# Turning the adjacency with the DMA engines instead of TensorE, through a bf16 copy in DRAM

## The chip, the cores and the metric

The kernel runs on one core of a Trainium2 chip. The metric is device time in microseconds (us) of one execution. All times are medians of 4 executions, except for the kernel before: it ran 4 times to compare with the changed kernel (3 of them were known before the prediction) and 7 times beside each group of experiments.

## The reference, cut to what matters

Sixteen batches of 1024 nodes with 256 features go through four graph attention layers. Every layer of a batch uses the same adjacency, an int32 matrix of 1024 x 1024.

```python
_a = jax.random.bernoulli(key, 0.00390625, (16, 1024, 1024))
_a = jnp.logical_or(_a, jnp.swapaxes(_a, -1, -2))     # symmetric
adj = jnp.logical_or(_a, jnp.eye(1024, dtype=bool)).astype(jnp.int32)
# simplified; each layer:  h = max(layernorm(x), 0)
#              x = x + attention(h, adj)    softmax over j, masked where adj[i, j] == 0
```

The inputs are symmetric, but the reference does not promise it, so the kernel turns each block of adjacency. An unturned block still gives the right result here.

## The kernel before

The kernel keeps a turned uint8 mask of each batch in SBUF, the memory that all engines work in; TensorE writes its results to PSUM, from where another engine copies them. `load(b)` fetches it, 128 rows at a time. It is a generator: the program calls it step by step, one block after each of eight groups of layer 3 of batch b-2.

```python
    def load(b: int):
        xs[b] = nodes.tile([P, NI, D], F32, name="x_b")
        nc.sync.dma_start(xs[b], x[b].rearrange("(i p) f -> p i f", p=P))
        mask = masks[b] = nodes.tile([P, NI, N], U8, name="mask")
        fetched = {}

        def fetch(i: int):
            fetched[i] = adjs.tile([P, N], BF, name="adj_i")        # 3 buffers
            nc.gpsimd.dma_start(fetched[i], adj[b, ts(i, P), :])    # casts int32 to bf16
        for i in range(AHEAD):                                      # AHEAD = 2
            fetch(i)
        yield
        for i in range(NI):                                         # NI = 8
            if i + AHEAD < NI:
                fetch(i + AHEAD)
            adj_i = fetched.pop(i)
            every = wide.tile([P, N], BF, name="wide")
            nc.scalar.activation(                                   # a check of the values
                every, adj_i, AF.Square, bias=minus_half, accum_out=squares[:, b, i : i + 1]
            )
            turned = psum.tile([P, NI, P], BF, name="misc", bufs=3)
            for j in range(NI):
                nc.tensor.transpose(turned[:, j, :], adj_i[:, ts(j, P)], ident_b)
            nc.scalar.copy(mask[:, :, ts(i, P)], turned)
            yield
    ...
    def batch(b: int):
        ...
        coming = load(b + 2) if b + 2 < B else iter(())
        ...
        V = yield from attend(0, V, finish0, 1)      # layer 0, projecting for layer 1
        V = yield from attend(1, V, finish, 2)
        V3 = yield from attend(2, V, finish, 3)
        ...
        for n in range(H * NH):                      # layer 3: 8 groups
            ...
            nc.scalar.copy(sums, accT)
            next(coming, None)                       # one block of batch b + 2
            ...
```

Two streams of batches, even and odd, run half a batch apart. A scheduler then orders the instructions of each engine with a simulation of its own, so the order on an engine is not the order of the program. `tc.keep_in_program_order(ins)` keeps an instruction behind everything that the program gave its engine earlier. Each engine works through its built order without overtaking.

Of the kernel before, what the change touches and what calls it, by code (L numbers as in the profile page):

```python
# [33 lines left out]
BF = mybir.dt.bfloat16  # L34
# [7 lines left out]
P = 128  # L42
# [17 lines left out]
def short_path(ctx: ExitStack, tc: tile.TileContext, ins: dict, out: bass.AP, bad: bass.AP):  # L60

    nc = tc.nc
    x, adj = ins["x"], ins["adj"]
    B, N, D = x.shape
    H, T, E = ins["L3_a_src"].shape
    NI = N // P
# [10 lines left out]
    adjs = ctx.enter_context(tc.tile_pool(name="adjs", bufs=3))  # L77
    wide = ctx.enter_context(tc.tile_pool(name="wide", bufs=2))
    psum = ctx.enter_context(tc.tile_pool(name="psum", bufs=2, space=bass.MemoryType.PSUM))

    ident = const.tile([P, P], F32, name="ident")
    make_identity(nc, ident)
    ident_b = const.tile([P, P], BF, name="ident_b")
# [8 lines left out]


    xs, masks = {}, {}

    def load(b: int):

        xs[b] = nodes.tile([P, NI, D], F32, name="x_b")
        nc.sync.dma_start(xs[b], x[b].rearrange("(i p) f -> p i f", p=P))
        mask = masks[b] = nodes.tile([P, NI, N], U8, name="mask")  # L100
        fetched = {}

        def fetch(i: int):

            fetched[i] = adjs.tile([P, N], BF, name="adj_i")
            nc.gpsimd.dma_start(fetched[i], adj[b, ts(i, P), :])  # L106

        for i in range(AHEAD):
            fetch(i)
        yield  # L110
        for i in range(NI):
# [5 lines that stand above are left out]
            nc.scalar.activation(  # L117
                every, adj_i, AF.Square, bias=minus_half, accum_out=squares[:, b, i : i + 1]
            )
            turned = psum.tile([P, NI, P], BF, name="misc", bufs=3)  # L120
            for j in range(NI):
                nc.tensor.transpose(turned[:, j, :], adj_i[:, ts(j, P)], ident_b)  # L122
            nc.scalar.copy(mask[:, :, ts(i, P)], turned)
            yield

    edges = ctx.enter_context(tc.tile_pool(name="edges", bufs=4))
# [104 lines left out]
    def project(l: int, xb: bass.AP, pair: int, evict):  # L231


        mv = small.tile([P, 2, nc.vector.BN_AGGR_DIM], F32, name="mv")
        for n in range(2):
            stats = small.tile([P, nc.vector.BN_STATS_DIM], F32, name="stats")
            nc.vector.bn_stats(stats, xb[:, 2 * pair + n, :])  # L237
            nc.vector.bn_aggr(mv[:, n, :], stats)
        rstd = inverse_root(mv[:, :, 1], 2, LN_EPS)
        centered = work.tile([P, 2, D], F32, name="centered", bufs=3)  # L240
        for n in range(2):
            nc.vector.tensor_scalar(  # L242
                centered[:, n, :], xb[:, 2 * pair + n, :], mv[:, n, 0:1], 0.0,
                op0=ALU.subtract, op1=ALU.max,
            )
        yield 0.5
        turned = psum.tile([P, NK, 2 * P], F32, name="misc", bufs=3)
        for n in range(2):
            for k in range(NK):
                nc.tensor.transpose(turned[:, k, ts(n, P)], centered[:, n, ts(k, P)], ident)  # L250
        hT = wide.tile([P, NK, 2 * P], F32, name="hT", bufs=3)
        nc.scalar.copy(hT, turned)  # L252
        yield 1.0
        for n in range(2):
            projected = psum.tile([P, D + EXT[l]], F32, name="projected")
            for k in range(NK):
                nc.tensor.matmul(  # L257
                    projected, hT[:, k, ts(n, P)], W[l][:, k, :],
                    start=(k == 0), stop=(k == NK - 1),
                )  # L260
            evict(2 * pair + n, projected, rstd[:, n : n + 1])
        yield 2.5

    def weigh(column, c, mask: bass.AP, op, half: int, into: list):


        turned = psum.tile([P, HALF], F32, name="misc", bufs=3)
        for n in range(NG):
            nc.tensor.transpose(  # L269
                turned[:, ts(n, P)], column(half * NG + n).to_broadcast([P, P]), ident  # L270
            )
        r = rows.tile([P, HALF], F32, name="row")
        nc.scalar.copy(r, turned)  # L273
        w = edges.tile([P, NI, HALF], F32, name="weights")
        into.append(w)
        for j in range(NI):
            nc.vector.scalar_tensor_tensor(  # L277
                w[:, j, :], r, c(j), mask[:, j, ts(half, HALF)], op0=op, op1=ALU.mult
            )
            if j % 4 == 3:  # L280
                yield 1.5
# [17 lines left out]
    def batch(b: int):  # L299
        xb, mask = xs.pop(b), masks.pop(b)  # L300
        if b == 0:
            next(preparing)
        coming = load(b + 2) if b + 2 < B else iter(())

        def begin(l: int):

            V = nodes.tile([P, NI, H, E + 1], F32, name="V").rearrange("p i h e -> p i (h e)")

            def evict(i: int, projected: bass.AP, rstd: bass.AP):
                nc.scalar.activation(V[:, i, D : D + 3], projected[:, D:], AF.Exp, scale=rstd)  # L310
                if l == 2:
                    nc.scalar.mul(V[:, i, :D], projected[:, :D], rstd)
                else:
                    nc.vector.tensor_scalar(  # L314
                        V[:, i, :D], projected[:, :D], rstd, V[:, i, D : D + 1],
                        op0=ALU.mult, op1=ALU.mult,
                    )

            return V, evict

# [3 lines left out]
        def begin3():  # L324
            h3 = last["h3"] = single.tile([P, NI, D], F32, name="h3")
            V3 = nodes.tile([P, NI, H, E + 1], F32, name="V")
            ex = last["ex"] = small.tile([P, NI, 3 * H], F32, name="ex", bufs=2)

            def evict3(i: int, projected: bass.AP, rstd: bass.AP):
                nc.scalar.activation(ex[:, i, :], projected[:, D:], AF.Exp, scale=rstd)  # L330
                nc.scalar.mul(h3[:, i, :], projected[:, :D], rstd)
                q = ex[:, i, :H].unsqueeze(2)
                nc.gpsimd.tensor_mul(
                    V3[:, i, :, :E], h3[:, i, :].rearrange("p (h e) -> p h e", h=H),
                    q.to_broadcast([P, H, E]),
                )
                nc.gpsimd.tensor_copy(V3[:, i, :, E:], q)
                nc.gpsimd.tensor_add(xb[:, i, :], xb[:, i, :], beta)

            return V3, evict3  # L340

        def attend(l: int, V: bass.AP, finish, then: int):

            op = ALU.min if l == 1 else ALU.max
            halves = []
            weighing = [
                weigh(
                    lambda i: V[:, i, D + 2 : D + 3], lambda j: V[:, j, D + 1 : D + 2],
                    mask, op, half, halves,
                )  # L350
                for half in range(NH)
            ]
            yield from weighing[0]
            following = begin(then) if then < 3 else begin3()
            steps = iter(())
            for i in range(NI):
                t = next(weighing[1], None)
                if t:
                    yield t
                acc = psum.tile([P, HALF], F32, name="acc", bufs=3)[:, : D + 1]  # L360
                w = halves[i // NG]
                for j in range(NI):
                    nc.tensor.matmul(  # L363
                        acc, w[:, j, ts(i % NG, P)], V[:, j, : D + 1],
                        start=(j == 0), stop=(j == NI - 1),
                    )
                finish(i, acc)
                yield 3.6
                if i % 2 == 1:

                    yield from steps
                    steps = project(then, xb, i // 2, following[1])
                yield from islice(steps, 1)
            yield 1.0
            yield from steps
            return following[0]
# [8 lines left out]
        def finish(i: int, acc: bass.AP):  # L385
            add_elu(xb[:, i, :], acc)
# [10 lines left out]
                pass  # L397
        V = yield from attend(0, V, finish0, 1)
        V = yield from attend(1, V, finish, 2)
        V3 = yield from attend(2, V, finish, 3)  # L400


# [37 lines left out]
        for n in range(H * NH):  # L440
# [5 lines left out]
            for j in range(NI):  # L446
                nc.tensor.matmul(  # L447
                    accT, V3[:, j, h, :], w[:, j, :], start=(j == 0), stop=(j == NI - 1)
                )
# [29 lines left out]
    def stream(first: int):  # L479
# [3 lines left out]
        for b in range(first, B, 2):  # L483
            yield from batch(b)

    loading, preparing = load(0), prepare()
    next(loading)
    next(preparing)
    streams = [[0.0, stream(0)], [LAG, stream(1)]]
# [384 lines left out]
```

## Time and profile before

| | before |
|---|---|
| time, median of 3 (range) | 3267.69 us (3262.37 to 3269.32) |
| span of the profiled execution | 3263.2 us |
| TensorE busy, idle | 3075.4 us, 187.8 us |
| VectorE, ScalarE, GpSimd busy | 2546.2, 969.4, 1085.1 us |
| granted TensorE clock, mean | 0.986 |

"Busy" of an engine is the time covered by its instructions; idle is the span less that. TensorE is the bound: it idles 5.8% of the span. The lines behind the table stand in the prediction, with their reading. A group's line there has line, engine, operation, shapes and count, then busy us and mean ns of one, then the idle time before it and what ended that. A wait's line has who waited, for what, then us in total, times and the longest.

### The profile page before, as it was taken

To read this page: it belongs to the slowest core of one execution; us is meant where nothing else is said; L and a number is where in the kernel's file an instruction comes from. 1 tells how busy PE (TensorE), PEld (TensorE's weight loads), DVE (VectorE), ACT (ScalarE), POOL (GpSimd) and SP (SyncE) were. 2 spreads that over 40 slices of the span, in tenths; PEclk is the share of its full clock that TensorE was granted. 3 is DMA by queue.
4 is the path that set the end of the run, shared out by engine and by line. 5 is a ranking of instruction groups with operands and counts; after the bars stand their busy time and mean duration, and the time that the engine had idled before them with its cause. 6 is when DMAs were issued, how large, how long until landed. Compare 5 with 4: busy or idle time off the path is not lost.

```text
span 3263.2 us, 38469 instructions
## 1 busy us (share of the span) xinstructions
PE 3075.4 (94%) x13702; PEld 2130.8 (65%) x13702; DVE 2546.2 (78%) x6140; ACT 969.4 (30%) x2081; POOL 1085.1 (33%) x1286
## 2 busy tenths in 40 slices
PE   7999999999999999999999999999999999999987
PEld 6765766657666676666766567675676766767562
DVE  5778787777887778877788877888778777787867
ACT  3423323232332323323233232322323223232121
POOL 1323424233242332423334233342323424233242
PEclk8999999999999999999999999999999999999999
DMA  4101101011010111100111010110101101000000
GB/s 105 27 4 17 33 14 39 7 17 30 14 39 7 17 30 17 36 11 13 30 17 36 10 21 23 16 36 13 39 4 17 33 13 40 4 14 13 1 13 14
DMA packets 55958, 72.13 MB, mean 22 GB/s; under 512 B 5072, under 2 KB 38992, under 8 KB 55760
## 3 DMA queue, kind: packets, MB, share of 16 engines
q0 software_dynamic: 18432, 33.56, 7.1%
q1 hardware_dynamic: 37328, 36.05, 3.6%
q8 instruction: 110, 1.80, 0.2%
q14 instruction: 88, 0.72, 0.1%
HBM read 86.38 MB, written 16.78 MB: 32 GB/s over the span
## 4 chain that ended last, share of the span: by engine, by line
PE 71%; DVE 17%; POOL 6%; issue 3%; ACT 2%; DMA 1%; POOLq 0%; ACTq 0%; SPq 0%; DVEq 0%
PE acc L363 32%; PE acc L447 22%; PE projected L257 11%; DVE weights L277 7%; PE misc L250 2%; PE misc L269 2%; POOL x_b L297 2%; DVE centered L242 2%; DVE stats L237 2%; POOL rstd L228 1%; PE misc L122 1%; DVE above L295 1%; DVE above L296 1%; POOL y L427 1%; ACT below L293 1%
## 5 line engine op out<-in xcount | busy, mean ns | idle before, releaser
L363 PE MATMUL acc<-V,weights 128*128 128x257 f32 x6144 | 1444.7, 385 | 9.5 <-DVE weights L277 8.1
L363 PEld LDWEIGHTS acc<-V,weights 128*128 128x128 f32 x6144 | 1142.9, 191 | 207.2 <-DVE weights L277 39.6
L447 PE MATMUL acc<-weights,V 128*65 128x512 f32 x2048 | 909.6, 592 | 0.3 <-DVE weights L277 0.3
L277 DVE SCALAR_TENSOR_TENSOR weights<-row,ex,mask 128x512 f32<-128x512 f32 x1024 | 744.5, 775 | 36.5 <-ACT row L273 36.5
L277 DVE SCALAR_TENSOR_TENSOR weights<-row,V,mask 128x512 f32<-128x512 f32 x768 | 593.0, 814 | 49.5 <-ACT row L273 48.1
L228 POOL TENSOR_TENSOR rstd<-rstd,minus_half 128x2 f32<-128x2 f32 (+1 forms) x320 | 330.4, 1035 | 882.4 <-DVE rstd L227 834.0
L447 PEld LDWEIGHTS acc<-weights,V 128*65 128x65 f32 x2048 | 278.7, 138 | 497.1 <-issue 475.5
L257 PE MATMUL projected<-W,hT 128*128 128x259 f32 (+1 forms) x2048 | 522.1, 397 | 40.6 <-DVE V L314 24.7
L257 PEld LDWEIGHTS projected<-W,hT 128*128 128x128 f32 x2048 | 387.4, 195 | 135.6 <-DVE V L314 37.0
L297 POOL TENSOR_TENSOR x_b<-x_b,above 128x256 f32<-128x256 f32 x256 | 222.0, 867 | 478.2 <-DVE above L296 440.7
L293 ACT ACTIVATE below<-acc,inv 128x256 f32<-128x256 f32 x256 | 121.0, 473 | 657.3 <-DVE inv L286 460.8
L237 DVE BATCH_NORM_STATS2 stats<-x_b 128x6 f32<-128x256 f32 x512 | 209.1, 415 | 128.4 <-POOL x_b L297 120.5
L250 PE MATMUL misc<-ident,centered 128*128 128x128 f32 x1024 | 168.9, 281 | 89.6 <-DVE centered L242 76.3
L252 ACT COPY hT<-misc 128x512 f32<-128x512 f32 x256 | 147.2, 588 | 302.4 <-PE misc L250 301.6
L242 DVE TENSOR_SCALAR centered<-x_b,mv 128x256 f32<-128x256 f32 x512 | 229.4, 451 | 4.7
L451 ACT COPY sums<-acc 65x512 f32<-65x512 f32 x128 | 74.1, 579 | 511.4 <-PE acc L447 509.9
L250 PEld LDWEIGHTS misc<-ident,centered 128*128 128x128 f32 x1024 | 120.5, 143 | 143.0 <-DVE centered L242 114.2
L273 ACT COPY row<-misc 128x512 f32<-128x512 f32 x224 | 129.8, 587 | 197.5 <-PE misc L269 197.3
L106 POOL DMA_DIRECT2D adj_i<-in_adj_dram x128 | 77.6, 606 | 284.9 <-ACT sums L451 215.4
L295 DVE TENSOR_SCALAR above<-acc,inv 128x256 f32<-128x256 f32 x256 | 122.6, 479 | 62.1 <-ACT below L293 60.9
L412 POOL TENSOR_TENSOR y<-y,bias 128x512 f32<-128x512 f32 x64 | 90.2, 1410 | 234.0 <-DVE y L459 215.7
L310 ACT ACTIVATE V<-projected,rstd 128x3 f32<-128x3 f32 x384 | 99.1, 262 | 226.0 <-PE projected L257 226.0
(70 smaller groups left out, 2307.8 us busy)
## 6 DMA issues: line engine op xcount, KB each, us to landing
adj_i<-in_adj_dram POOLq DMA_DIRECT2D x128, 256.0 KB, 3.8
x_b<-in_x_dram SPq DMA_DIRECT2D x16, 1024.0 KB, 7.8
out_dram<-y SPq DMA_DIRECT2D x32, 512.0 KB, 3.8
W<-in_L_gnn_W_dram SPq DMA_DIRECT2D x3, 256.0 KB, 9.6
weights<-in_L_gnn_a_dram SPq DMA_DIRECT2D x3, 256.0 KB, 9.6
W<-in_L_gnn_W_dram SPq DMA_DIRECT2D x2, 128.0 KB, 10.3
weights<-in_L_gnn_a_src_dram SPq DMA_DIRECT2D x1, 128.0 KB, 8.8
weights<-in_L_gnn_a_dst_dram SPq DMA_DIRECT2D x1, 128.0 KB, 5.2
```

Source lines behind the costliest of these rows:

```text
L228: nc.gpsimd.tensor_tensor(r, r, minus_half.to_broadcast([P, n]), op=ALU.pow)
L237: nc.vector.bn_stats(stats, xb[:, 2 * pair + n, :])
L242: nc.vector.tensor_scalar(centered[:, n, :], xb[:, 2 * pair + n, :], mv[:, n, 0:1], 0.0, op0=ALU.subtract, op1=ALU.max,)
L250: nc.tensor.transpose(turned[:, k, ts(n, P)], centered[:, n, ts(k, P)], ident)
L252: nc.scalar.copy(hT, turned)
L257: nc.tensor.matmul(projected, hT[:, k, ts(n, P)], W[l][:, k, :], start=(k == 0), stop=(k == NK - 1),)
L277: nc.vector.scalar_tensor_tensor(w[:, j, :], r, c(j), mask[:, j, ts(half, HALF)], op0=op, op1=ALU.mult)
L293: nc.scalar.activation(below, acc[:, :D], AF.Exp, scale=inv)
L295: nc.vector.tensor_scalar(above, acc[:, :D], inv, 0.0, op0=ALU.mult, op1=ALU.max)
L297: nc.gpsimd.tensor_add(xi, xi, above)
L363: nc.tensor.matmul(acc, w[:, j, ts(i % NG, P)], V[:, j, : D + 1], start=(j == 0), stop=(j == NI - 1),)
L447: nc.tensor.matmul(accT, V3[:, j, h, :], w[:, j, :], start=(j == 0), stop=(j == NI - 1))
```

## The change

The intent is to take the turning from TensorE. For batches 2 to 15, four casting transfers on GpSimd write the whole matrix as bf16 to a scratch in DRAM. The program issues them before layer 2 of batch b-2, and holds them in program order on GpSimd. In layer 3, Sync loads each block with a transposing DMA, and ScalarE copies it straight from SBUF into the mask. The first two batches stay as they were.

```diff
+    narrows = [dram.tile([N, N], BF, name=f"narrow{n}") for n in range(2)]
     def load(b: int):
+        by_dma = b >= 2
+        if by_dma:
+            for q in range(4):
+                quarter = ts(q, N // 4)
+                cast = nc.gpsimd.dma_start(narrows[b % 2][quarter, :], adj[b, quarter, :])
+                tc.keep_in_program_order(cast)
+        yield
 ...
-            nc.gpsimd.dma_start(fetched[i], adj[b, ts(i, P), :])
+            if by_dma:
+                nc.sync.dma_start_transpose(fetched[i], narrows[b % 2][:, ts(i, P)])
+            else:
+                nc.gpsimd.dma_start(fetched[i], adj[b, ts(i, P), :])
 ...
-            turned = psum.tile([P, NI, P], BF, name="misc", bufs=3)
-            for j in range(NI):
-                nc.tensor.transpose(turned[:, j, :], adj_i[:, ts(j, P)], ident_b)
-            nc.scalar.copy(mask[:, :, ts(i, P)], turned)
+            if by_dma:
+                nc.scalar.copy(mask[:, i, :], adj_i)
+            else:
+                (the four lines above)
 ...
         V = yield from attend(1, V, finish, 2)
+        next(coming, None)
         V3 = yield from attend(2, V, finish, 3)
```

More of the change, by code (lines that the diff above doesn't have):

```diff
@@ L79, in short_path @@
     psum = ctx.enter_context(tc.tile_pool(name="psum", bufs=2, space=bass.MemoryType.PSUM))
+    dram = ctx.enter_context(tc.tile_pool(name="dram", bufs=1, space=bass.MemoryType.DRAM))
     ident = const.tile([P, P], F32, name="ident")
@@ L119, in load @@
             )
-            turned = psum.tile([P, NI, P], BF, name="misc", bufs=3)
-            for j in range(NI):
-                nc.tensor.transpose(turned[:, j, :], adj_i[:, ts(j, P)], ident_b)
-            nc.scalar.copy(mask[:, :, ts(i, P)], turned)
+            if by_dma:
+                nc.scalar.copy(mask[:, i, :], adj_i)
+            else:
+                turned = psum.tile([P, NI, P], BF, name="misc", bufs=3)
+                for j in range(NI):
+                    nc.tensor.transpose(turned[:, j, :], adj_i[:, ts(j, P)], ident_b)
+                nc.scalar.copy(mask[:, :, ts(i, P)], turned)
             yield
@@ L486, in short_path @@
     loading, preparing = load(0), prepare()
+    next(loading)
     next(loading)
```

## The prediction

> **What bounds the kernel now.** I read the busy shares first, then the windows of one period, then TensorE's timeline, then the waits. The times before are 3262 to 3269 us, median 3267.69.
>
> ```profile
> PE 3075.4 (94%) x13702; PEld 2130.8 (65%) x13702; DVE 2546.2 (78%) x6140; ACT 969.4 (30%) x2081; POOL 1085.1 (33%) x1286
> q0 software_dynamic: 18432, 33.56, 7.1%
> ```
>
> TensorE is busy 94% of the span and VectorE 78%; ScalarE and the DMA engines are mostly idle. Two batches are in flight, half a batch apart, so stores of `y` leave every 200 us. The windows (busy us of TensorE, its weight loads, VectorE, ScalarE, GpSimd, then granted clock) of two such periods:
>
> ```profile
> 1556.00:1756.00 200.00, 192.87 (x864) 133.55 (x865) 161.38 (x394) 60.86 (x131) 73.31 (x88) 1.00 0.11 23
> 1756.00:1957.00 201.00, 190.36 (x850) 131.92 (x848) 156.61 (x369) 59.85 (x130) 63.64 (x73) 0.99 0.11 21
> ```
>
> TensorE idles 7 to 11 us of each 200, at full clock. It sets the period, so the work taken from it is worth nearly its issue time, and any wait put into its order costs nearly its length.
>
> The timeline around two groups of eight turning transposes (L122), columns start, duration, engine, line:
>
> ```profile
> 1628.06 7.03 PE L447 MATMUL acc<-weights,V 128*65 128x512 f32 x16
> 1634.93 0.61 PE L122 MATMUL misc<-ident_b,adj_i 128*128 128x128 bf16 x8
> 1635.37 0.61 PE L250 MATMUL misc<-ident,centered 128*128 128x128 f32 x4
> 1635.82 0.60 PE L269 MATMUL misc<-ident,V 128*128 128x128 f32 x4
> 1636.67 0.46 PE L456 MATMUL misc<-ident,sums 65*128 65x65 f32 x4 [0.26 <-ACT mask L123]
> ...
> 1650.90 0.61 PE L122 MATMUL misc<-ident_b,adj_i 128*128 128x128 bf16 x8
> 1651.35 0.87 PE L363 MATMUL acc<-V,weights 128*128 128x257 f32 x3
> ```
>
> From the start of a group to the start of the next work it is 0.44 to 0.45 us: eight times 55 ns. The duration of 0.61 us overlaps what follows, so the busy sum overstates the cost. The groups by shape and the waits:
>
> ```profile
> L122 PE MATMUL misc<-ident_b,adj_i 128*128 128x128 bf16 x1024 | 79.9, 222 | 9.9 <-DMA adj_i<-in_adj_dram 7.5 <-ACT mask L123 1.9
> L123 ACT CAST mask<-misc 128x1024 uint8<-128x1024 bf16 x128 | 129.0, 1011 | 1.5 <-PE misc L122 1.4
> PE misc L456 <- ACT mask L123: 11.7, 14, 1.4
> POOL adj_i L106 <- ACT sums L451: 215.4, 51, 14.8
> ```
>
> The third line: fourteen times (once a batch) L456 waits for a PSUM buffer that still holds a turned block. The fourth: GpSimd's in-order queue stands 215 us before a load, because a buffer is not free; this rarely ends TensorE's idle time.
>
> **What the Trainium skill says.** "TensorE: Matmul & The Clock Gate", Part 4: a 128x128 bf16 transpose was about 275 ns in one kernel. The trace has 219 ns median, and 55 ns from start to start; I use the latter. "DMA: Bandwidth & Descriptors", SWDGE vs HWDGE vs iDMA: a DMA that casts must come from GpSimd, one that transposes from Sync or Scalar. The trace agrees for the casting loads (software queue); no transposing DMA is in it. The same page, Two DMAs through the same engine are not ordered: a DMA that reads what another wrote must wait for that one's completion semaphore, so turning cannot begin before the casts have landed. The same page, Latency and other measured facts: a DMA transpose reached 261 GB/s in one kernel. No trace here shows it.
>
> **The change, part by part.** Batches 2 to 15, 14 of 16, with 8 blocks each: 112 groups.
>
> 1. Removed from TensorE: 112 x 0.445 = 50 us of issue time (the busy sum would fall by 112 x 0.624 = 70 us).
> 2. Removed PSUM waits: L456 behind L123, 11.7 us, nearly all in the turned batches: 10 us.
> 3. ScalarE: 112 casts now read SBUF instead of PSUM, near 1.0 to 1.1 us each as before (L117, same width from SBUF, takes 1.15). Not the bound; 0.
> 4. GpSimd: 112 issues of 0.6 us become 56, and the 285 us of standing before loads mostly go. Worth perhaps 3 us, since GpSimd is on 6% of the chain.
>    Gain so far: about 62 us.
> 5. Added: each batch needs 4 MiB of int32 cast to 2 MiB of bf16 in DRAM, then eight transposes of 256 KiB. The old loads used 7.1% of 16 engines: 0.071 x 3263 / 128 = 1.81 us of all engines for 512 KiB read. Eight times that is 14.5 us for a batch; with some 2 us of latency (3.8 us measured to landing, less 1.8), the casts need about 16 us from first issue. Estimate for one transpose: 256 KiB at the skill's 261 GB/s is 1.0 us, plus 2 us of latency and about 1.5 us for issue and semaphores: 4.5 us. So about 21 us from the first cast to a turned block.
>
> Bandwidth is no problem. Position is. I compared the built kernels' instruction orders. The program puts the turning in layer 3, but the order that was built does not: the first two mask copies of a batch stand on ScalarE right at the start of layer 2, a few instructions after the casts on GpSimd, and ScalarE works in order.
>
> For odd batches (3, 5, ... 15: seven) GpSimd issues the casts straight after the inverse root of the last pair of layer 2's projection. ScalarE evicts the first block of that pair, and its next instruction is the mask copy that needs cast and turn. The second block's eviction stands behind it. TensorE's next-but-one group (the row transposes) needs that eviction. Between the end of the `acc` that the inverse root depends on and that projection, TensorE has 4 + 4 L257 passes (1.9 us), 4 small transposes (0.25), one L447 group (6.9), 0.44 + 0.44 + 0.25, and 0.9 of projection: 11 us. The chain from `acc` to the issued cast (inverse, below, above, addition, statistics, root) took about 7 us in the same place before. So the casts begin about 4 us before ScalarE arrives; it stands 21 - 4 - 1 = 16 us, and TensorE almost as long. Issue overlap could shorten it; I take 13 us: 7 x 13 = 91 us.
>
> For even batches (2, 4, ... 14: seven) the casts follow the root in `center`, and ScalarE arrives some 2 us later, so it stands about 17 us. But TensorE has work: two `acc` groups, which VectorE feeds at about 0.75 us a block, and one L447 of 6.9 us, some 16 us in all. Exposed with the backlog of two copies (2 us): 4 us each: 28 us.
>
> Later pairs of copies stand one or two instructions after the Square that frees their buffer; a transpose of 4.5 us makes ScalarE stand 2 to 4 us, mostly hidden by 7-us L447 groups: 42 pairs, 0.4 us each: 15 us.
>
> Sum: 3268 - 62 + 91 + 28 + 15 = 3340 us.
>
> **Rivals.**
> - *Plain gain.* The casts land sooner, or TensorE's slack hides the wait: 3268 - 62 = 3206, and up to 3195 if the busy sum of 70 us is the right measure. For it: DMA is 11% busy in the period, and ScalarE is at 30%. Against it: the order has no slack in odd batches, and 4 MiB cannot be read in 5 us at the 300 to 390 GB/s that the DMA view shows when it is busy.
> - *VectorE takes over.* With TensorE at 189 of 200 us and VectorE at 161, stretches of layer 3 (36 of 40 us busy at 1636 to 1676) may leave only two thirds of the gain: about 3225. It cannot make the kernel slower.
> - *Slow transposes.* If 256-byte rows of DRAM make a transpose take 10 us or more, every pair of copies holds ScalarE 6 to 9 us, and half of that reaches TensorE: 56 x 4 = 220 us more than the gain: 3450 and up. Only the skill's figure speaks against it.
>
> **Range and chances.** The gain side is known within 15 us. The cost side is not: the exposed wait of an odd batch may be 5 to 18 us and of an even one 0 to 10, so 35 to 196 us, plus the unknown transposes. The centre is 3338; 8 times in 10 it should be 3210 to 3440. Faster by over 2% (below 3202) needs the full gain and no exposed wait: 0.12. Within 2% (to 3333): 0.39. Slower: 0.49.
>
> **What would show each step.** TensorE's busy sum falls by about 70 us and L122 to 128 matmuls. The PSUM wait on L123 is gone. New: ScalarE's mask copy waiting for the DMA of `adj_i`, fourteen long waits of 10 to 20 us, and TensorE idle at the row transposes behind ScalarE's `V` eviction in odd batches. The period grows beyond 200 us. I am wrong if the casts land within 8 us of issue, if the transposes take far more than 5 us, or if TensorE's idle time does not grow.

## The result, and the profile after

The changed kernel takes 3340.37 us (3337.85 to 3342.42). The ratio to before is 1.0225 (95% interval 1.0207 to 1.0243): 2.2% slower. Ratios here and below are the mean time of one kernel's fast runs over the mean of the other's of the same rounds, so they are not quite the ratio of the medians quoted. All outputs are right.

Line numbers moved by 16 or so. The row transposes of L269 are L285 now, the `acc` groups of L363 are L379, and L123 is L134 for the turned batches. From the page of the changed kernel, the busy times and the two DMA queues (packets, MB, share of 16 engines):

```profile
PE 3032.0 (91%) x12806; PEld 2101.8 (63%) x12806; DVE 2543.9 (76%) x6140; ACT 968.8 (29%) x2081; POOL 1038.8 (31%) x1230
q1 hardware_dynamic: 155600, 65.42, 8.0%
q0 software_dynamic: 4096, 33.56, 5.1%
```

TensorE has 896 matmuls fewer and 43.4 us less busy time. Yet the span grew by 77.6 us, so its idle time grew by 121.0 us, to 308.8 us. The transfers stay far from full. The changed kernel's windows of two periods from store to store show it (columns as in the prediction):

```profile
1556.00:1769.00 213.00, 196.41 (x839) 136.62 (x838) 166.77 (x395) 65.31 (x142) 66.29 (x81) 0.98 0.14 33
1769.00:1968.00 199.00, 178.55 (x746) 122.82 (x745) 150.26 (x365) 55.51 (x118) 62.39 (x71) 0.97 0.14 30
```

Two periods take 412 us, 11 more than before, and TensorE idles 16.6 and 20.5 us in them. The changed kernel's waits say on what:

```profile
ACT mask L134 <- DMA adj_i<-narrow: 269.4, 54, 17.7
PE misc L285 <- ACT V L326: 74.8, 7, 12.1
PE acc L379 <- DVE above L311: 36.7, 6, 6.3
```

ScalarE stands 54 times for turned blocks, up to 17.7 us. TensorE's two largest new waits come seven and six times; there are seven odd and seven even turned batches. The wait of L456 (now L473) for a PSUM buffer held by a mask copy is gone. The changed kernel's timeline at an odd batch, where layer 2 begins:

```profile
733.54 0.81 POOL L244 TENSOR_TENSOR rstd<-rstd,minus_half 128x2 f32<-128x2 f32 x1 [1.85 <-DVE rstd L243]
734.21 2.07 POOL L106 DMA_DIRECT2D narrow<-in_adj_dram  x4
...
740.21 0.26 ACT L326 ACTIVATE V<-projected,rstd 128x3 f32<-128x3 f32 x1 [0.81 <-PE projected L273]
...
747.71 2.50 SPq L117 DMA_TRANSPOSE adj_i<-narrow  x2
751.29 1.04 ACT L134 CAST mask<-adj_i 128x1024 uint8<-128x1024 bf16 x1 [10.45 <-DMA adj_i<-narrow]
752.24 0.26 ACT L326 ACTIVATE V<-projected,rstd 128x3 f32<-128x3 f32 x1
...
752.55 0.48 PE L285 MATMUL misc<-ident,V 128*128 128x128 f32 x1 [10.37 <-ACT V L326]
```

Read it from the top. The root is done and the casts go out at 734.2. ScalarE evicts one block at 740.2 (copies it out of PSUM); what comes next on it is the mask copy. The casts land only at about 747.7, when Sync issues the transposes, and the first block lands 3.6 us later. ScalarE stands 10.45 us, the next eviction stands behind it, and TensorE waits 10.37 us for that eviction. The same at an even batch:

```profile
526.20 2.05 POOL L106 DMA_DIRECT2D narrow<-in_adj_dram  x4
...
539.75 2.50 SPq L117 DMA_TRANSPOSE adj_i<-narrow  x2
543.40 2.01 ACT L134 CAST mask<-adj_i 128x1024 uint8<-128x1024 bf16 x2 [17.67 <-DMA adj_i<-narrow]
...
546.45 5.34 PE L379 MATMUL acc<-V,weights 128*128 128x257 f32 x16 [6.17 <-DVE above L311]
```

ScalarE stands 17.67 us, but TensorE has other work and waits only 6.17 us. Then sixteen matmuls take 5.34 us. Windows of the changed kernel, two around the even wait and then three around the odd one, show the granted clock (third figure from the end):

```profile
528.00:540.00 12.00, 11.89 (x42) 6.47 (x42) 6.80 (x13) 0.00 (x0) 0.25 (x1) 1.00 0.68 142
546.40:552.00 5.60, 5.34 (x16) 4.13 (x16) 4.30 (x12) 0.94 (x2) 3.91 (x4) 0.70 0.00 0
...
730.00:734.00 4.00, 4.00 (x16) 1.74 (x15) 3.29 (x16) 1.18 (x4) 1.29 (x3) 1.00 0.00 0
...
752.50:757.00 4.50, 4.45 (x12) 3.61 (x13) 3.77 (x6) 1.78 (x3) 1.27 (x1) 0.50 0.00 0
...
762.00:770.00 8.00, 8.00 (x40) 6.71 (x38) 6.55 (x9) 5.81 (x11) 5.51 (x4) 1.00 0.35 68
```

The mean clock is 1.00 before the even wait and 0.70 after it; it is 1.00 before the odd wait, 0.50 after it and 1.00 again some 10 us later. The Trainium skill, "TensorE: Matmul & The Clock Gate", Part 1, says that TensorE falls back to half clock after about 3.4 us without work and needs as long a busy stretch to recover. The trace agrees as far as these windows go: after waits of 6.17 and 10.37 us the clock is down, so a wait is paid again in part, in slower matmuls. Groups and transfers of the changed kernel:

```profile
L138 PE MATMUL misc<-ident_b,adj_i 128*128 128x128 bf16 x128 | 12.5, 252 | 16.2 <-DMA adj_i<-in_adj_dram 12.7 <-ACT mask L139 3.0 <-ACT row L289 0.5
narrow<-in_adj_dram POOLq DMA_DIRECT2D x56, 512.0 KB, 9.4
adj_i<-narrow SPq DMA_TRANSPOSE x112, 3.4
```

The turning group fell from 79.9 to 12.5 us. A cast landed in 9.4 us (median, among four), a transpose in 3.4 us.

### The profile page after: what moved, and what is told of

The parts are those of the page before. It is cut to its first block, busy times and chain, and to the rows that moved or that the text cites. A ratio compares the mean times of both kernels' runs of the same rounds, so it can differ in the third digit from the quotient of the medians.

```text
span 3340.8 us, 36798 instructions
## 1 busy us (share of the span) xinstructions
PE 3032.0 (91%) x12806; PEld 2101.8 (63%) x12806; DVE 2543.9 (76%) x6140; ACT 968.8 (29%) x2081; POOL 1038.8 (31%) x1230
## 4 chain that ended last, share of the span: by engine, by line
PE 47%; DVE 33%; DMA 8%; POOL 5%; ACT 3%; issue 3%; SPq 0%; ACTq 0%; POOLq 0%; DVEq 0%
PE acc L379 22%; DVE weights L293 18%; PE acc L464 13%; PE projected L273 8%; DMA narrow<-in_adj_dram 5%; DMA adj_i<-narrow 3%; PE misc L266 2%; DVE stats L253 2%; DVE centered L258 2%; DVE V L330 1%; POOL x_b L313 1%; DVE above L311 1%; PE misc L285 1%; POOL y L429 1%; DVE above L312 1%
## 5 line engine op out<-in xcount | busy, mean ns | idle before, releaser
L379 PE MATMUL acc<-V,weights 128*128 128x257 f32 x6144 | 1445.0, 388 | 44.3 <-DVE above L311 36.7
L379 PEld LDWEIGHTS acc<-V,weights 128*128 128x128 f32 x6144 | 1168.7, 195 | 230.9 <-issue 57.9
L293 DVE SCALAR_TENSOR_TENSOR weights<-row,ex,mask 128x512 f32<-128x512 f32 x1024 | 758.4, 783 | 1.8 <-ACT row L289 1.8
L293 DVE SCALAR_TENSOR_TENSOR weights<-row,V,mask 128x512 f32<-128x512 f32 x768 | 572.6, 795 | 82.9 <-ACT V L326 60.9
L244 POOL TENSOR_TENSOR rstd<-rstd,minus_half 128x2 f32<-128x2 f32 (+1 forms) x320 | 323.4, 1012 | 886.1 <-DVE rstd L243 879.6
L253 DVE BATCH_NORM_STATS2 stats<-x_b 128x6 f32<-128x256 f32 x512 | 208.9, 415 | 91.2 <-POOL x_b L313 82.1
L134 ACT CAST mask<-adj_i 128x1024 uint8<-128x1024 bf16 x112 | 116.5, 1046 | 270.2 <-DMA adj_i<-narrow 269.4
L330 DVE TENSOR_SCALAR V<-projected,rstd,V 128x256 f32<-128x256 f32 x256 | 135.1, 535 | 65.5 <-ACT V L326 65.1
```

What stands on the lines that cost most here:

```text
L244: nc.gpsimd.tensor_tensor(r, r, minus_half.to_broadcast([P, n]), op=ALU.pow)
L253: nc.vector.bn_stats(stats, xb[:, 2 * pair + n, :])
L293: nc.vector.scalar_tensor_tensor(w[:, j, :], r, c(j), mask[:, j, ts(half, HALF)], op0=op, op1=ALU.mult)
L330: nc.vector.tensor_scalar(V[:, i, :D], projected[:, :D], rstd, V[:, i, D : D + 1], op0=ALU.mult, op1=ALU.mult,)
L379: nc.tensor.matmul(acc, w[:, j, ts(i % NG, P)], V[:, j, : D + 1], start=(j == 0), stop=(j == NI - 1),)
```

## The experiments

My theory after reading the trace is the prediction's. TensorE gains its turning time. It loses more because ScalarE stands at mask copies that the scheduler put ahead of their data. Rivals: (a) the DMA traffic itself slows other work; (b) turning costs TensorE less than I thought, so the gain is small; (c) the transposing DMA is slow; (d) the scheduler built a worse order of the other instructions. Twelve kernels ran, four each on three chips. The kernel before ran beside them, with medians of 3267.84, 3267.88 and 3266.09 us, so I compare across the three.

### noturn: the kernel before, without the turning

```diff
-            turned = ... eight transposes ...
-            nc.scalar.copy(mask[:, :, ts(i, P)], turned)
+            if b >= 2:
+                nc.scalar.copy(mask[:, i, :], adj_i)
+            else:
+                (as before)
```

> The kernel before, but for batches 2 to 15 the loaded rows are copied to the mask without being turned (this adjacency is symmetric, so the result stays right; it isolates the gain of not turning on TensorE, with the old loads and no casts to DRAM). My theory: 112 groups of 0.445 us, 10 us of PSUM waits, no new waits: 3268 - 60 = 3208, between 3200 and 3218. Rival 'VectorE takes over': only two thirds, 3228 or more. Rival 'the busy sum of 70 us is the right measure': 3185 to 3198.

Measured: 3283.36 us (3279.99 to 3285.92), ratio 1.0044 (1.0027 to 1.0061). I expected 3208, a clear miss. Two waits of this kernel tell why:

```profile
ACT mask L121 <- DMA adj_i<-in_adj_dram: 186.0, 103, 4.7
POOL adj_i L106 <- ACT wide L117: 206.6, 42, 6.1
```

Without the turning in between, the scheduler puts the copies where ScalarE meets loads under way: 103 waits. So noturn is no clean measure of the gain. noturnpinned (below) is the same kernel with the copies held, and 54 us faster: copies brought forward do harm without any casts to DRAM.

### layer1: the casts a layer earlier

```diff
+        next(coming, None)
         V = yield from attend(1, V, finish, 2)
-        next(coming, None)
         V3 = yield from attend(2, V, finish, 3)
```

> The changed kernel with its casts issued at the start of layer 1 instead of layer 2; same transfers, same instructions, nearly the same order on ScalarE. My theory (the long waits of ScalarE for the casts reach TensorE, about 11 us in odd batches and 6 in even ones): both go, and 3340 - 75 - 37 = 3228, between 3205 and 3240; the waits of the mask copies for the DMA fall from 269 us to under 110, and the granted clock returns to 0.98 or more. Rival 'the added traffic or the transposes slow everything': stays at 3325 or more. Rival 'another instruction order is at fault': stays above 3300.

Measured: 3214.82 us (3209.37 to 3216.97), ratio 0.9834 (0.9818 to 0.9851), as expected; only the waits, 112.7 us, are a little above the 110 that I set. The granted clock is back at 0.983. Its wait of ScalarE:

```profile
ACT mask L134 <- DMA adj_i<-narrow: 112.7, 60, 6.2
```

No wait is longer than 6.2 us, and TensorE's idle time at the row transposes fell from 75.1 to 0.5 us. Earlier casts alone turn a loss of 2.2% into a gain of 1.7%. Compared place by place in the two traces, 14 of TensorE's 12806 matmuls stand elsewhere than in the changed kernel, so rival (d) does not explain its loss.

### pinned: the mask copies held in program order

```diff
-                nc.scalar.copy(mask[:, i, :], adj_i)
+                copied = nc.scalar.copy(mask[:, i, :], adj_i)
+                tc.keep_in_program_order(copied)
```

> The changed kernel with its casts in layer 2 as they are, but each mask copy held behind the ScalarE instructions that the program has before it, so that the scheduler can't bring it forward to the start of layer 2. My theory (the place of the copies is what costs, not the casts in layer 2): the first copy comes some 10 ScalarE instructions later, so most of the wait is gone: 3215 to 3260. If the casts themselves or their traffic cost the time: 3320 or more.

Measured: 3169.55 us (3168.54 to 3171.76), ratio 0.9702 (0.9685 to 0.9718), better than expected: I had the copies come some 10 instructions later, and they come about 100 us later. The casts and transposes stay where the change put them, and nearly all that moved is on ScalarE: in the traces 98 of TensorE's 12806 matmuls and 264 of VectorE's 6140 instructions stand elsewhere. No mask copy waits for a DMA any more. The timeline of pinned at the same even batch:

```profile
511.84 2.05 POOL L106 DMA_DIRECT2D narrow<-in_adj_dram  x4
525.40 16.34 SPq L117 DMA_TRANSPOSE adj_i<-narrow  x3
...
626.26 1.05 ACT L134 CAST mask<-adj_i 128x1024 uint8<-128x1024 bf16 x1
```

The casts again take 13.6 us until the transposes go out. But the batch's first copy comes at 626.3, in layer 3 and 100 us later (the copies that I left out, up to 545 us, are the last of the batch loaded before). No wait for these transfers is left when no engine meets them before they have landed.

### layer1twice: the cast traffic doubled

layer1 with four equal casts more for each batch, into a scratch that nobody reads.

```diff
+                cast = nc.gpsimd.dma_start(spare[quarter, :], adj[b, quarter, :])
+                tc.keep_in_program_order(cast)
```

> As layer1, and before each batch's four casts four more of the same size into a spare array that nobody reads: twice the cast traffic, with time to land. My theory (traffic costs nothing while nobody waits for it): within 10 us of layer1. Rival 'traffic costs': 3340 - 3268 + 60 = about 130 us more than the gain for one set, so at least 60 us above layer1.

Measured: 3217.70 us (3216.06 to 3220.86), ratio 0.9845, against 3214.82 for layer1. The engines' orders are the same in both traces. Twice the casts cost about 3 us, within the spread of the runs; rival (a) said 60 or more and falls.

### beforepinned and noturnpinned: where did the 98 us come from?

pinned is 98 us under before, but the prediction's gain was 62. Holding copies in order may help before too, so I did it there. noturnpinned is noturn with the same line.

```diff
-            nc.scalar.copy(mask[:, :, ts(i, P)], turned)
+            copied = nc.scalar.copy(mask[:, :, ts(i, P)], turned)
+            if b >= 2:
+                tc.keep_in_program_order(copied)
```

> The kernel before with its mask copies of batches 2 to 15 held in program order on ScalarE, nothing else. If holding the copies in order is itself worth what 'pinned' gained beyond my 62 us (36 us), this is 3225 to 3240. If that gain belongs to the turning that left TensorE, this is 3258 to 3278: there the copies wait for TensorE's transposes anyway.

Measured: 3255.09 us (3251.97 to 3257.93), ratio 0.9960 (0.9944 to 0.9977): 13 us, a little more than I allowed. The kernel before paid a little for copies out of place too: TensorE's idle time falls from 187.8 to 179.0 us in the profiled executions.

> 'noturn' with its mask copies held in program order. My theory after the first runs: 'noturn' was slow because copies stood on ScalarE right at the landing of their load (186 us of waits); held back, they wait for nothing, and this is the whole gain of not turning, with no DMA turning at all: 3160 to 3185, equal to 'pinned' within 12 us. If the gain is only the 60 us that I worked out: 3200 to 3215, and 'pinned' has something else.

Measured: 3229.16 us (3228.55 to 3229.91), ratio 0.9883 (0.9866 to 0.9899). I expected 3160 to 3185: a miss. The mask waits are gone, yet 60 us separate it from pinned, though both have the same TensorE work. Either the loads on GpSimd cost that, or the order that the scheduler built: in the traces 5140 of TensorE's 12806 matmuls stand elsewhere than in pinned.

### pinnedrest and pinnedtwo: the long waits and the short ones apart

The first two copies of a batch are those at the start of layer 2; the other six come later. pinnedrest holds only the six, pinnedtwo only the two.

```diff
                 copied = nc.scalar.copy(mask[:, i, :], adj_i)
-                tc.keep_in_program_order(copied)
+                if i >= 2:                       # pinnedtwo: if i < 2
+                    tc.keep_in_program_order(copied)
```

> As 'pinned', but only blocks 2 to 7 of each batch are held in order; the first two copies stay where the change has them, at the start of layer 2 behind the casts. Measures the later pairs alone: layer1 minus pinned says 45 us, so 3340 - 45 = 3295, between 3280 and 3312; my prediction's 15 us says 3325.

Measured: 3304.24 us (3301.05 to 3304.99), as expected. So the long waits alone cost 3304.2 - 3169.6 = 135 us. The wait and the busy times of pinnedrest, then the busy times of pinned:

```profile
ACT mask L134 <- DMA adj_i<-narrow: 171.3, 13, 16.5
PE 3031.2 (92%) x12806; PEld 2103.0 (64%) x12806; DVE 2530.8 (77%) x6140; ACT 967.1 (29%) x2081; POOL 1031.4 (31%) x1230
```

```profile
PE 2996.3 (95%) x12806; PEld 2084.0 (66%) x12806; DVE 2528.5 (80%) x6140; ACT 967.8 (31%) x2081; POOL 1039.5 (33%) x1230
```

With the same matmuls, TensorE is busy 34.9 us longer in pinnedrest. The rest of the 132.5 us between the two spans (3299.4 and 3166.9), 97.6 us, is idle time. I read the busy part as the slower clock after the waits: the mean clock is 0.968 against 0.984, and the `acc` groups that follow the waits (L379 in the changed kernel) account for 34.8 us of it, busy 1450.0 us in pinnedrest and 1415.2 us in pinned.

> As 'pinned', but only the first two copies of each batch are held in order; the later ones stay as the change has them. The long waits for the casts go, the pairs' short ones stay: like layer1, 3215, between 3200 and 3235.

Measured: 3206.22 us (3202.57 to 3209.38), as expected. So the later pairs alone cost 37 us. Unrounded, the two parts make 134.7 + 36.7 = 171.4 us, and the changed kernel is 170.8 us slower than pinned: they add up, within the spread of the runs. The wait of pinnedtwo:

```profile
ACT mask L134 <- DMA adj_i<-narrow: 82.1, 40, 6.4
```

### plainpinned, poolpinned, turnpinned, layer1pinned: one factor at a time

plainpinned is pinned with a plain transfer instead of the transposing one. poolpinned issues that transfer on GpSimd instead of Sync. turnpinned gives the turning back to TensorE. I compared the built orders: TensorE, ScalarE, VectorE and GpSimd have the same in plainpinned as in pinned. In poolpinned TensorE and ScalarE have it too, VectorE but for two neighbours.

```diff
-                nc.sync.dma_start_transpose(fetched[i], narrows[b % 2][:, ts(i, P)])
+                nc.sync.dma_start(fetched[i], narrows[b % 2][ts(i, P), :])      # plainpinned
+                nc.gpsimd.dma_start(fetched[i], narrows[b % 2][ts(i, P), :])    # poolpinned
```

> The kernel of run pinned with one thing altered: Sync loads each bf16 block from the DRAM scratch by a plain transfer instead of a transposing one (adjacency is symmetric, so the result stays right). The orders of TensorE, VectorE, ScalarE and GpSimd as built are the same as in pinned. If the transposing transfer costs nothing that reaches the end: 3170 us, 3160 to 3180. If pinned is held back by the turning in the DMA engines (3.4 us to landing): a little under 3160.

Measured: 3169.73 us (3165.63 to 3170.89). With the copies held, the transposing form costs nothing in the total, and rival (c) falls for pinned. Where ScalarE does wait for a transpose, as in pinnedtwo, its 3.4 us to landing are part of the wait; no run has plain loads there, so how much of the 37 us a faster load would save is not measured.

> plainpinned with one thing altered: the plain loads from the DRAM scratch are issued by GpSimd instead of Sync. TensorE and ScalarE have the same orders as in plainpinned, VectorE but for two neighbours; on GpSimd the loads stand between its computations again, each after the Square that frees its buffer. Theory (the gain of the change beyond the turning comes from taking the waiting loads out of GpSimd's in-order queue): about 3229 us, the level of noturnpinned, with GpSimd standing some 200 us before loads; 3205 to 3250. Rival (noturnpinned is slower only because the scheduler put the other instructions in another order): within 10 us of plainpinned, about 3170.

Measured: 3190.13 us (3188.94 to 3192.96), ratio to before 0.9772 (0.9755 to 0.9788), against 0.9704 (0.9688 to 0.9721) for plainpinned. Neither theory was right: the issuing engine is worth 20 us, not 60. TensorE's order is the same in both, yet 13.6 us of the 20 are longer TensorE busy time (3010.9 against 2997.3 us), at a mean clock of 0.979 against 0.984 in the profiled executions. Nor did GpSimd stand 200 us: its largest wait before these loads is 31.9 us in total. The busy times of poolpinned (those of plainpinned follow below):

```profile
PE 3010.9 (94%) x12806; PEld 2095.3 (66%) x12806; DVE 2541.7 (80%) x6140; ACT 967.6 (30%) x2081; POOL 1103.5 (35%) x1342
```

turnpinned has the plain transfer on Sync, and this:

```diff
-                copied = nc.scalar.copy(mask[:, i, :], adj_i)
+            turned = psum.tile([P, NI, P], BF, name="misc", bufs=3)
+            for j in range(NI):
+                nc.tensor.transpose(turned[:, j, :], adj_i[:, ts(j, P)], ident_b)
+            copied = nc.scalar.copy(mask[:, :, ts(i, P)], turned)
```

> plainpinned with the turning given back to TensorE: bf16 blocks come over Sync from the DRAM scratch, eight transposes into PSUM, ScalarE's copy from there held in program order. Theory (GpSimd's queue is worth some 60 us, the turning on TensorE some 26 to 60): 3195 to 3230. Rival (the turning on TensorE costs all that beforepinned lost against pinned, 85 us): about 3255.

Measured: 3229.05 us (3226.74 to 3232.67), ratio 0.9890 (0.9874 to 0.9907). The turning on TensorE is worth 3229 - 3170 = 59 us, near the 60 of the prediction, so rival (b) falls. The busy times of turnpinned, then of plainpinned:

```profile
PE 3053.8 (95%) x13702; PEld 2127.8 (66%) x13702; DVE 2537.2 (79%) x6140; ACT 969.0 (30%) x2081; POOL 1042.3 (32%) x1230
```

```profile
PE 2997.3 (95%) x12806; PEld 2084.4 (66%) x12806; DVE 2527.7 (80%) x6140; ACT 968.3 (31%) x2081; POOL 1039.1 (33%) x1230
```

896 matmuls less are 56.5 us less of busy time, nearly all of the 59. The busy times of beforepinned, and the transposes of `sums` in beforepinned and in turnpinned, for the account below:

```profile
PE 3076.3 (94%) x13702; PEld 2133.3 (66%) x13702; DVE 2546.8 (78%) x6140; ACT 969.3 (30%) x2081; POOL 1079.6 (33%) x1286
L458 PE MATMUL misc<-ident,sums 65*128 65x65 f32 x512 | 54.7, 227 | 18.0 <-ACT mask L123 11.7 <-ACT sums L453 6.2
L472 PE MATMUL misc<-ident,sums 65*128 65x65 f32 x512 | 53.1, 226 | 8.0 <-ACT sums L467 6.2 <-ACT mask L136 1.8
```

layer1pinned joins the two remedies:

> Both remedies together: casts issued in layer 1 as in run layer1, and every mask copy held in program order as in run pinned. If the wait for casts is wholly gone in pinned, nothing is left to gain: 3160 to 3180. If casts in the middle of layer 2 still cost something there: under 3160.

Measured: 3170.13 us (3168.71 to 3171.30). With the copies held, nothing is left to gain from earlier casts. pinned, plainpinned and layer1pinned are equal and beat both kernels. Of the three, plainpinned leans on the symmetric input; pinned and layer1pinned are general; pinned is 3.0% faster than before.

## Why the prediction was right or wrong, point by point

The total was right: 3338 predicted, 3340 measured. The mechanism was the predicted one, shown from both sides: moving the casts away from the copies (layer1) or the copies away from the casts (pinned) removes the loss. That the number was met within 2 us is luck: the gain is 98 us where the prediction had 62, the loss 171 us where it had 134, and the two errors, of 36 and 37 us, cancelled. The terms, with the runs that measure them (the first three measured terms go step by step from before to plainpinned, which equals pinned, so they must add up to its gain; that the two losses add up is a test):

| term | predicted, us | measured, us | from |
|---|---|---|---|
| steps 1 and 2, turning and PSUM waits | -60 | -59 (see below) | turnpinned to plainpinned |
| step 4, loads leave GpSimd | -3 | -26, with 10 of step 2 | beforepinned to turnpinned |
| copies out of place in before | none | -13 | before to beforepinned |
| long waits at layer 2 | +91 + 28 | +135 | pinned to pinnedrest |
| later pairs | +15 | +37 | pinned to pinnedtwo |
| sum, from 3268 | 3340 (gain rounded to 62) | 3342 (measured 3340) | |

- **Steps 1 and 2** come out near, 59 us for 60, in part by luck. Step 1 was 50 us: to count 0.445 us from start to start, and not the 0.624 us of the busy sum, was near, but the busy time gave 56.5 us for 112 groups, 0.50 us each. Step 2's 10 us are not in the 59: the transposes of `sums` (L456 in the kernel before) wait 11.7 us for mask copies in beforepinned and 1.8 us in turnpinned, so these 10 us lie in the 26 us of the next row. "TensorE's busy sum falls by about 70" was wrong for the kernel as a whole, where it fell by 43.4. The turning group did fall by 67.4, but its busy time overlaps that of its neighbours (turnpinned to plainpinned, removing it gave 56.5), and the clock fell from 0.986 to 0.967.
- **Step 3** held: 112 mask copies from SBUF took 116.5 us, 1.04 each.
- **Step 4** was mis-sized: "worth perhaps 3 us, since GpSimd is on 6% of the chain". From beforepinned to turnpinned it is 26 us. That step also removes 10 us of step 2's wait, and it changes the source of the loads and the built order: 5876 of TensorE's 13702 matmuls stand elsewhere. Of the 28.7 us between the two spans, 22.5 us are TensorE busy time at the same clock of 0.985 (3076.3 and 3053.8 us), so most of it is not time in which TensorE stood idle. With the order held, the issuing engine alone is worth 20 us (poolpinned to plainpinned). The share of the chain that ended last (6%) was no measure of what issuing on GpSimd costs.
- **Step 5**, the length of the transfers, was near. The casts took 13.5 us, predicted 16. From the first cast to a turned block that ScalarE could use it took about 17 us, predicted 21. One transpose landed in 3.4 us, predicted 4.5; the 1.5 us for issue and semaphores in that estimate came from no trace.
- **The long waits** were predicted well in kind. In odd batches TensorE waited 74.8 us in seven, 10.7 each, where I took 13: in the batch shown the casts had a head start of 6.6 us on ScalarE (734.2 to 740.8), not 4, and the transfers took 17 us, not 21. In even ones it waited 36.7 us in six at L379, 6.1 each, where I took 4. What I left out is the clock: 34.9 us of longer busy time after the waits, in pinnedrest. That term of the sum was missing; the waits themselves came out a little below the 119 us predicted.
- **The later pairs** cost 37 us, not 15: "0.4 us each" was mis-sized, it is 0.9. Their mechanism was right: pinnedtwo still has ScalarE standing 82.1 us, 40 times. Of the 33.9 us between its span and that of pinned, 14.6 us are longer TensorE busy time.
- **Rivals.** The plain gain (3195 to 3206) is what comes once the waits are gone, and pinned even passes it. "VectorE takes over" (3225) did not show: pinned runs at 3170. The slow transposes did not come: 3.4 us, and no cost against plain loads.

What stays open: noturnpinned and poolpinned both load through GpSimd and turn nothing, yet differ by 39 us (3229 and 3190). They differ in the source of the loads, int32 with a cast or bf16 from DRAM, and in the built order of TensorE. No run separates these two. For the same reason the 26 us are not split fully. Nor is it shown why poolpinned's clock is lower.

## What to carry to other kernels

Before work moves to an engine with room, look where its consumer stands in the built order: an in-order engine that meets its data too early (here by 10 to 18 us, 13 times, and by shorter stretches 41 times) makes every engine behind it pay, here 171 us against a gain of 98. The cure is cheap: give the transfer a head start, or hold the consumer back. A wait of TensorE can cost more than its length: the 13 waits of pinnedrest, about 6 to 11 us each and 110.8 us in all, came with 34.9 us of longer busy time at a lower mean clock.

## What the Trainium skill lacked or had wrong

- "TensorE: Matmul & The Clock Gate" gives a bf16 transpose about 275 ns, as a duration. Its Part 1 gives 55.6 ns from start to start for back-to-back matmuls of 128 columns; that transposes among other matmuls reach this is not said: here they take 55 ns from start to start, and each group of eight removed saved 0.50 us of busy time (56.5 us for 112).
- "DMA: Bandwidth & Descriptors" gives only a rate for the transposing DMA. Missing is the time of one of 256 KiB to landing: 3.4 us median in the changed kernel, against 2.6 us for the plain load of the same size in turnpinned, with no difference in the total (3169.55 and 3169.73 us).
- The same page, under Issuing engines are not separate DMA queues, says that another issuing engine only saves the issue time on the sequencer, usually small. The runs do not contradict it, but a size is missing: moving 112 plain loads from GpSimd to Sync took 64.4 us off GpSimd's busy time (1103.5 and 1039.1 us) and was worth 20 us of 3190 (poolpinned and plainpinned).
- No page that I read gives the time of a casting transfer from DRAM to DRAM: 4 MiB of int32 to 2 MiB of bf16, in four transfers, took 13.5 us from the first issue until the dependent transfers went out.
